# A CIN kernel on one Trainium2 core: the last stretch of matmuls put in another order, with other PSUM banks for two quadrant products

## The chip, the cores and the metric

The kernel runs on one core of a Trainium2 chip. The time is the device time of one execution in microseconds (us), and the median of several runs is compared. Beside these times there is one execution recorded by the profiler. Its engines are called PE (matrix multiplication; PEld are its weight loads), DVE (vector), ACT (scalar), POOL and SP (whose queue issues most of the loads).

## What is computed

The reference is a compressed interaction network over 1024 samples with 64 fields of 16 numbers each:

```python
x0 = h = x                                   # (1024, 64, 16)
for i in range(3):
    z = einsum('bfe,bge->bfge', x0, h)       # all products of two fields
    y = einsum('oc,bce->boe', W[i], z.reshape(B, -1, e)) + b[i]
    x_i, h = (y[:, :64], y[:, 64:]) if i != 2 else (y, y)
    xs.append(x_i)
return sum(concatenate(xs, 1), axis=2) @ fc_w.T + fc_b     # (1024, 1)
```

Everything is fp32. After the sum over the 16 numbers only one value for each sample is left, so the kernel folds the weights of the last layers with fc_w before the main loop. What remains for each sample and number e: h, the 64 upper outputs of layer 1, a sum over the products of fields x_f x_g with weights from W0; q, 64 sums over the same products with weights made from W1, W2 and fc_w; and smaller terms in x. The result is a sum over h times q and over the terms in x.

## The kernel before, in words

**Tiling.** The samples form 32 chunks of 32, so a chunk is 512 columns (32 samples by 16 numbers)[...]. The products of fields of a chunk are made as four blocks `z`, each 128 rows by 4 tiles by 512 columns (`product`, L237, and `w_product`, L631). A product multiplies `xa`, the chunk with shifted rows, by one quarter `xb` of another arrangement of it; for most products ACT first copies `xb` to a PSUM bank of the tag "y" (`second`, L551), of which there are two. PE multiplies 16 tiles of z by `w_all`, whose columns 0 to 63 give h and 64 to 127 give q. A matmul thus fills 64 output rows: half 0 is rows 0 to 63 of a bank, half 1 is rows 64 to 127. Two matmuls of different halves can run at a time. All main matmuls go through `mm`, L524, so the profile shows them at L525, told apart by their output's name.

**Stages.** Chunks 2, 3, 0 and 1 are the head, in which weights are still being made. Chunks 0, 1, 4 and 5 are finished plainly. Of chunks 2 and 3 only h is made there and kept in `hb`; their q is made at the end. Chunks 6 to 31 go as 13 pairs (`NPAIR`), numbered 3 to 15, in a scheme with seven half products instead of eight (Winograd's form of Strassen's): sums of blocks (T2, T3, B21, B22, X; on DVE and POOL) are multiplied by sums of weights (`ws`) into the banks alpha, delta (tag "acc", four banks) and beta (tag "set", two). Each pair is a window of 31 slots; a slot is a pair of 512-column matmuls.

**The last pair's leftovers.** A pair's window leaves over: one matmul into beta (`first_fill`, L715), eight of `late_run` and one with `vb` into alpha (L721), and four of `p4_run` into delta (L712, `LATE`). These run in the next pair's window. The last pair, number 15, has no next one, so they run in the stretch that the change touches, together with q of chunks 2 and 3. There, two of the eight late matmuls go to the free half of alpha's bank (`gamma`, L610) and are added later (`end_gamma`, L939).

**Quadrants.** For each chunk four smaller terms are taken by 64 by 64 matmuls, which use a quarter of the array each: `h_extra` (L564) and `v0x` (L571). For a pair this is `squares` (L725), at slot 30.2 of its window; for chunks 2 and 3 it is `end_squares` (L923). They read `e`, a chunk and its square (`square`, L179, on ACT).

**The end.** `end_q` (L912) multiplies the products of chunks 2 and 3 by the q weights into two banks: the first 384 columns (`ends[0]`, 24 samples) and, after them, the last 128 (`ends[1]`). Chunk 3 goes to half 0, chunk 2 to half 1. `end_extra` adds a term. DVE then finishes pair 15 (`end_pair`, L745: `w_hb`, `w_qa`, `w_ha`, twice `w_uu`, `x_v0x`, `sums`), adds up (`add_parts`, L947), and multiplies h by q of chunks 2 and 3 (`end_uu`, L933). PE sums over partitions with matmuls into `po` (`pools`, L953), placed in the middle of the 128-column matmuls; ACT and SP store the results. The last 8 samples of chunk 3 and of chunk 2 come last (L997 on).

**What sets the order.** The main part isn't written in order. `at(when, fn, ...)` (L515) puts a call into a list with a due time in slots, the list is sorted by it, and the calls then emit their instructions (L993). `zipped` (L518) gives two columns of jobs a slot for each row, the second column half a slot later. Each engine runs its own instructions in the order of emission; waits between engines, and for banks to become free, are put in by the framework. So the due times set an order, not times. In the end, `t` is the slot at which window 15 ends.

Of the kernel before, what the change touches and what calls it, by code (L numbers as in the profile page):

```python
# [37 lines left out]
F32 = mybir.dt.float32  # L38
# [8 lines left out]
N = CB * E  # L47
# [5 lines left out]
NT = NI * NJ  # L53
# [10 lines left out]
NPAIR = NCH // 2 - 3  # L64
GROUPS = [(j, i) for j in range(2) for i in range(NI)]
LATE = 4


@with_exitstack
def cin_kernel(ctx, tc, xra, xrb, wh, w0r, w1h, w2t, wx1, wx0, vec, out):  # L70
# [5 lines left out]
    ps = ctx.enter_context(tc.tile_pool(name="ps", bufs=2, space=bass.MemoryType.PSUM))  # L76
# [3 lines left out]
    def const_tile(name, shape):  # L80
        return const.tile(shape, F32, tag=name, name=name)
# [149 lines left out]
    hb = const_tile("hb", [128, NF // 2, N])  # L231
# [136 lines left out]
    for h in range(2):  # L368
        at = slice(32 * h, 32 * h + 32)
# [145 lines left out]
    def at(when, fn, *args, **flags):  # L515
        ops.append((when, len(ops), fn, args, flags))
# [7 lines left out]
    def mm(out, w, rhs, start=False, stop=False):  # L524
        nc.tensor.matmul(out, w, rhs, start=start, stop=stop, skip_group_check=True)  # L525
# [30 lines left out]
    def plain_product(when, c, j):  # L556
        at(when - 2.6, second, c, j)
        at(when, product, c, j, uses=NI)

    def q_extra(c, w, out=None):  # L560
        out = accs[c][halves[1 - c % 2]] if out is None else out[halves[c % 2]]
        mm(out, w, es[c])

    def h_extra(c, out=None, start=False):  # L564
        out = accs[c] if out is None else out
        mm(out[halves[c % 2]], w0ds[halves[1]], es[c][halves[1]], start=start)

    def new_y(k, tag):
        ys[k] = ps.tile([128, N], F32, tag=tag, name=f"y_{k}", bufs=4 if tag == "acc" else 2)

    def v0x(c, tag):  # L571
        if c // 2 not in ys:
            new_y(c // 2, tag)
        mm(ys[c // 2][halves[c % 2]], v0[halves[0]], es[c][halves[0]], start=True, stop=True)
# [47 lines left out]
    def w_run(p, out, w, name, start=False, at_t=0, order=GROUPS):  # L622
        return [
            (w_job, p, out, w, j * NI + i + at_t, name, start and n == 0)
            for n, (j, i) in enumerate(order)
        ]
# [85 lines left out]
    def p4_run(p):  # L712
        return w_run(p, delta, wh_all, "T2", at_t=2 * NI)

    def first_fill(p):  # L715
        return [(lambda: q_extra(p["a"], va, p["beta"]),)] + p4_run(p)[-LATE : -LATE // 2]

    def second_fill(p):
        return p4_run(p)[-LATE // 2 :]

    def late_run(p, out=alpha, first=0, last=2 * NI):  # L721
        jobs = w_run(p, out, s4, "B22", out is gamma)[first:last]
        return jobs if last < 2 * NI else jobs + [(lambda: q_extra(p["b"], vb, p["alpha"]),)]
# [8 lines left out]
    def window(t, p, fill, late, pad=[], order=GROUPS[NI:] + GROUPS[:NI], quads=30.2):  # L732
# [4 lines left out]
            w_run(p, delta, s3, "T3", True) + late + w_run(p, beta, wq_all, "B21", True, 2 * NI)  # L737
            + pad + p4_run(p)[:-LATE],
        )
# [5 lines left out]
    def end_pair(t, p, whens):  # L745
        hb_, qa, uub, ha, uua, xv, add = whens
        at(t + hb_, w_hb, p)
        at(t + qa, w_qa, p)
        at(t + uub, w_uu, p, alpha, "A", snaps[2])
        at(t + ha, w_ha, p)  # L750
        at(t + uua, w_uu, p, delta, "O", snaps[0])
        at(t + xv, x_v0x, p["k"])
        at(t + add, sums, p["k"])
# [79 lines left out]
    for n in range(NPAIR):  # L833
# [6 lines left out]
        t = T0 + SPAN * n  # L840
# [12 lines left out]
        else:  # L853
            q = pairs[-2]
# [46 lines left out]

    t, q = T0 + SPAN * NPAIR, pairs[-1]
    first, cuts = slice(0, CUT), (slice(0, E * CUT), slice(E * CUT, N))
    ends = []

    def new_ends():
        for n, cols in enumerate(cuts):
# [13 lines left out]
        mm(ends[n][halves[1 - c % 2]], va, es[c][:, cuts[n]])  # L921

    def end_squares():  # L923
        hx = ps.tile([128, N], F32, tag="set", name="hx")
        for c in (2, 3):
            h_extra(c, hx, True)
            v0x(c, "set")
        h = hb[:, 1, :]
        nc.vector.tensor_tensor(h, hx, h, ALU.add)
        for n in range(2):  # L930
            nc.scalar.copy(snaps[3][halves[1 - n]], h[halves[n]])
# [28 lines left out]
    for n in (2, 3):  # L960
        at(t - 34 + 6 * (n - 2), load_xa, n)
        at(t - 33.5 + 6 * (n - 2), load_xb, n)
        at(t - 13 + n / 10, load_e, n)
        at(t, square, n)
    at(t - 12, load_xx, 1)
    for when, c, j in ((-21.4, 2, 0), (-18.6, 3, 0), (-15.8, 2, 1), (-12.2, 3, 1), (-6.1, 2, 2), (-2, 3, 2)):
        plain_product(t + when, c, j)
    for when, c in ((-5, 2), (0, 3)):
        at(t + when, product, c, NJ - 1, engine=nc.gpsimd, uses=NI)
    end_pair(t, q, (0.7, 4.5, 13.8, 13.3, 13.5, 9.5, 14.5))  # L970
    at(t + 10.5, end_gamma)
    at(t - 0.1, new_ends)
    zipped(
        t,
        first_fill(q)[:1] + late_run(q, gamma, 0, 2) + [(end_q, 3, m, 0) for m in range(6)]
        + p4_run(q)[-LATE:] + [(end_q, 3, m, 0) for m in range(6, NT)] + [(end_extra, 3, 0)],
        [(end_q, 2, m, 0) for m in range(3)] + late_run(q, first=2)
        + [(end_q, 2, m, 0) for m in range(3, NT)] + [(end_extra, 2, 0)],
    )
    at(t + 9.9, end_squares)  # L980
    at(t + 15, x_v0x, 1)
    at(t + 15.1, sums, 1, of=slice(1, 2))
    t += 25
    at(t - 8, add_parts)
    at(t - 0.2, end_uu, 0)
# [96 lines left out]
```

## Time and profile before

| What | us |
|---|---|
| median of 3 runs | 453.62 |
| lowest and highest run | 453.42, 455.04 |
| the profiled execution, its own time | 453.26 |
| its span in the trace | 451.4 |
| PE busy in the span | 446.7 (99%) |
| DVE, POOL, ACT busy | 392.8, 364.7, 116.6 |
| one 512-column matmul row on PE (alpha<-z,ws), mean | 0.592 |
| one weight load of 64 columns, mean | 0.137 |

The granted clock of TensorE was 1.0. In the timeline, a row gives its start in us from the beginning of the span, its duration, engine, line, operation, output and inputs with their shapes, how often it occurs in direct succession (x2), and in brackets how long its engine was idle before it and what ended that. The duration of a MATMUL row is modelled and includes its way through the array, so rows of one half overlap; the distance between starts is what a matmul costs. Each fp32 matmul of the program appears as two MATMUL rows.

### The profile page before, as it was taken

What the parts mean: (1) busy time and instruction counts of PE and PEld (TensorE: products, weight loads), DVE (VectorE), ACT (ScalarE), POOL (GpSimd) and SP (SyncE); (2) the same over time, 40 slices, a digit from 0 to 9 for tenths busy, and PEclk for the clock granted to TensorE, in tenths of its full rate; (3) what the DMA queues carried; (4) which work ended last, traced back from release to release, by engine and by line L of the source; (5) the groups of instructions that cost most, each with busy time, mean ns of one, the idle gap of its engine ahead of it and who ended that gap; (6) DMA issues with size and microseconds to landing.
All of it is one profiled execution on the core that took longest, in us unless ns stands there. A gap on an engine that the chain in (4) does not pass through costs nothing.

```text
span 451.4 us, 6068 instructions
## 1 busy us (share of the span) xinstructions
PE 446.7 (99%) x2302; PEld 162.4 (36%) x2302; DVE 392.8 (87%) x284; ACT 116.6 (26%) x215; POOL 364.7 (81%) x125
## 2 busy tenths in 40 slices
PE   8999999999999999999999999999999999999997
PEld 4565343333333333333333333333333333333345
DVE  4995599998999998999999898999989899997833
ACT  3162251332313114131311413131131213125011
POOL 5423688999997979799797979989797998979900
DMA  8996998397949296794939679493967849490500
GB/s 308 407 313 152 335 384 355 126 319 195 303 95 350 83 272 237 150 352 90 340 107 266 236 164 337 95 346 102 268 226 177 325 103 353 139 278 25 118 0 2
DMA packets 34484, 99.67 MB, mean 221 GB/s; under 512 B 6324, under 2 KB 6996, under 8 KB 27864
## 3 DMA queue, kind: packets, MB, share of 16 engines
q1 hardware_dynamic: 31800, 84.70, 52.1%
q0 software_dynamic: 1872, 13.63, 16.7%
q10 hardware_dynamic: 784, 0.95, 0.8%
q8 instruction: 18, 0.29, 0.3%
q14 instruction: 10, 0.08, 0.0%
HBM read 84.00 MB, written 1.64 MB: 190 GB/s over the span
## 4 chain that ended last, share of the span: by engine, by line
PE 84%; DVE 10%; issue 3%; DMA 1%; SPq 0%; ACT 0%; ACTq 0%
PE alpha L525 51%; PE delta L525 10%; PE acc L525 7%; PE acc L251 6%; DVE z L633 5%; PE q L525 3%; PE acc L269 3%; PE beta L525 3%; DMA z<-in_w0r 1%; DVE acc L293 1%; DVE uu L289 1%; DVE uu L681 1%; DVE delta L678 1%; DVE xp L639 1%; PE y L525 0%
## 5 line engine op out<-in xcount | busy, mean ns | idle before, releaser
L650 POOL TENSOR_TENSOR z<-z,z 128x2048 f32<-128x2048 f32 (+1 forms) x78 | 300.0, 3881 | 29.5 <-PE alpha L525 29.3
L633 DVE TENSOR_TENSOR z<-xa,xp 128x2048 f32<-128x2048 f32 x103 | 231.6, 2279 | 1.2
L525 PE MATMUL alpha<-z,ws 128*64 128x512 f32 x624 | 220.7, 592 | 0.0
L525 PEld LDWEIGHTS alpha<-z,ws 128*64 128x64 f32 x624 | 69.5, 137 | 120.5 <-issue 118.6
L525 PE MATMUL delta<-z,w_all 128*64 128x512 f32 x208 | 95.8, 593 | 0.0
L553 ACT COPY xp<-xb 128x512 f32<-128x512 f32 x88 | 51.5, 588 | 164.2 <-DVE z L633 141.6
L525 PE MATMUL alpha<-z,w_all 128*64 128x512 f32 x208 | 91.9, 595 | 0.8
L525 PE MATMUL delta<-z,ws 128*64 128x512 f32 x208 | 91.9, 595 | 0.0
L525 PE MATMUL beta<-z,w_all 128*64 128x512 f32 x208 | 91.6, 593 | 0.0
L241 DVE TENSOR_TENSOR z<-xa,xp 128x2048 f32<-128x2048 f32 (+2 forms) x23 | 45.1, 2003 | 6.2 <-ACT xp L553 5.4
L525 PEld LDWEIGHTS alpha<-z,w_all 128*64 128x64 f32 x208 | 27.6, 137 | 59.1 <-issue 48.5
L241 POOL TENSOR_TENSOR z<-xa,xb 128x2048 f32<-128x2048 f32 x6 | 27.6, 4669 | 19.9 <-DMA xb<-in_xrb 19.9
L525 PEld LDWEIGHTS delta<-z,w_all 128*64 128x64 f32 x208 | 28.2, 137 | 29.2 <-issue 28.3
L251 PE MATMUL acc<-z,w_all 128*64 128x256 f32 x256 | 28.9, 381 | 0.6 <-DVE z L241 0.4
L525 PE MATMUL acc<-z,w_all 128*64 128x512 f32 (+1 forms) x96 | 29.4, 594 | 0.0
L525 PEld LDWEIGHTS delta<-z,ws 128*64 128x64 f32 x208 | 27.6, 137 | 4.6 <-issue 4.3
L525 PEld LDWEIGHTS beta<-z,w_all 128*64 128x64 f32 x208 | 27.8, 137 | 0.0
L664 ACT ACTIVATE snap<-alpha,vs 64x512 f32<-64x512 f32 x13 | 8.9, 683 | 55.7 <-PE alpha L525 55.7
L251 PEld LDWEIGHTS acc<-z,w_all 128*64 128x64 f32 x256 | 18.1, 137 | 12.9 <-DVE z L241 2.0
L525 PE MATMUL q<-z,w_all 128*64 128x384 f32 (+1 forms) x128 | 20.0, 382 | 0.0
L681 DVE SCALAR_TENSOR_TENSOR uu<-alpha,snap 64x512 f32<-64x512 f32 x13 | 9.0, 689 | 12.6 <-PE alpha L525 12.6
L661 ACT COPY snap<-alpha 64x512 f32<-64x512 f32 x13 | 7.6, 581 | 47.8 <-PE delta L525 45.4
(117 smaller groups left out, 365.0 us busy)
## 6 DMA issues: line engine op xcount, KB each, us to landing
xa<-in_xra SPq DMA_DIRECT2D x32, 1024.0 KB, 9.1
xb<-in_xrb SPq DMA_DIRECT2D x128, 256.0 KB, 7.9
z<-z POOLq DMA_DIRECT2D x13, 1024.0 KB, 9.4
e<-in_xra SPq DMA_DIRECT2D x28, 128.0 KB, 7.6
xx<-in_xra SPq DMA_DIRECT2D x28, 128.0 KB, 6.9
z<-in_w2t SPq DMA_DIRECT2D x2, 1024.0 KB
z<-in_wx SPq DMA_DIRECT2D x2, 1024.0 KB, 8.5
z<-in_w1h SPq DMA_DIRECT2D x1, 1024.0 KB
```

Of the source, the lines that this page charges most:

```text
L241: engine.tensor_tensor(blocks[zs[c, j]][:, at, :], xas[c][:, at, :], xbs[c][j].unsqueeze(1).to_broadcast([128, last - first, N]), ALU.mult,)
L251: nc.tensor.matmul(accs[c][halves[n]], w_all[:, t, 0:64], blocks[zs[c, j]][:, i, n * H2 : (n + 1) * H2], start=(t == 0), stop=(j == last a ...
L269: nc.tensor.matmul(accs[c][halves[1 - c % 2]], w_all[:, t, 64:128], blocks[zs[c, j]][:, i, :], start=(t == 0), stop=False, skip_group_chec ...
L289: nc.vector.scalar_tensor_tensor(uu[:, to, :], ys[k], cx, xxs[k], ALU.add, ALU.mult)
L293: nc.vector.tensor_reduce(acc[rows, of, k, half], uu[rows, of if at is None else at, E * half.start : E * half.stop].rearrange("p k (b e) ...
L525: nc.tensor.matmul(out, w, rhs, start=start, stop=stop, skip_group_check=True)
L553: nc.scalar.copy(bank, xbs[c][j])
L633: engine.tensor_tensor(blocks[b], xas[c], xbs[c][j].unsqueeze(1).to_broadcast([128, NI, N]), ALU.mult)
L650: nc.gpsimd.tensor_tensor(*(blocks[b][:, first:last] for b in (o, x, y)), ALU.subtract if in1 == "T3" else ALU.add,)
L661: nc.scalar.copy(snaps[0][p["O"]], alpha(p))
L664: nc.scalar.activation(snaps[1][p["O"]], alpha(p), AF.Identity, bias=bh1[p["A"]])
L681: nc.vector.scalar_tensor_tensor(uu[p[out], 0], x(p), 1.0 / QS, factor[p[out]], ALU.mult, ALU.mult)
```

## The change

It gives the matmuls of the last stretch another order, in which the two halves always have matmuls of equal size side by side, and takes the quadrant matmuls of chunks 2 and 3 to the place directly behind those of pair 15. There are the same matmuls as before, of the same sizes. In detail:

- Column 0 of the stretch was: beta, two gamma, six `end_q` of chunk 3, four of `p4_run` (delta), ten `end_q`, the extra. Column 1 was: three `end_q` of chunk 2, six late ones and `vb` (alpha), thirteen `end_q`, the extra. Now both begin with seven `end_q` (`FIRST`); then come seven of 512 columns in each (beta, two gamma and four delta; six alpha and `vb`), then nine `end_q` and the extra in each.
- `end_squares` is split. The matmuls come before the stretch (due at t - 0.7) and write to banks of the tag "y" instead of "set". The addition of h and its copies (`end_h`) stay at t + 9.9.
- So that the y banks are free, the last product on DVE (chunk 3, block 2) is due at t - 4.2 instead of t - 2, which takes it ahead of the `sums` of pair 14; and `square` of chunks 2 and 3 is due at t - 6 instead of t.
- The due times of pair 15's last steps follow the new order.

```diff
+FIRST = 7
...
-    ends = []
+    ends, hxs = [], []
...
     def end_squares():
-        hx = ps.tile([128, N], F32, tag="set", name="hx")
+        hx = ps.tile([128, N], F32, tag="y", name="hx")
+        hxs.append(hx)
         for c in (2, 3):
             h_extra(c, hx, True)
-            v0x(c, "set")
-        h = hb[:, 1, :]
+            v0x(c, "y")
+
+    def end_h():
+        hx, h = hxs.pop(), hb[:, 1, :]
         nc.vector.tensor_tensor(h, hx, h, ALU.add)
         for n in range(2):
             nc.scalar.copy(snaps[3][halves[1 - n]], h[halves[n]])
...
-        at(t, square, n)
+        at(t - 6, square, n)
     at(t - 12, load_xx, 1)
-    for when, c, j in ((-21.4, 2, 0), (-18.6, 3, 0), (-15.8, 2, 1), (-12.2, 3, 1), (-6.1, 2, 2), (-2, 3, 2)):
+    for when, c, j in ((-21.4, 2, 0), (-18.6, 3, 0), (-15.8, 2, 1), (-12.2, 3, 1), (-6.1, 2, 2), (-4.2, 3, 2)):
         plain_product(t + when, c, j)
...
-    end_pair(t, q, (0.7, 4.5, 13.8, 13.3, 13.5, 9.5, 14.5))
-    at(t + 10.5, end_gamma)
+    end_pair(t, q, (0.7, FIRST + 1.3, 14.9, 14.5, 14.7, 9.5, 15.4))
+    at(t + 14.2, end_gamma)
     at(t - 0.1, new_ends)
     zipped(
         t,
-        first_fill(q)[:1] + late_run(q, gamma, 0, 2) + [(end_q, 3, m, 0) for m in range(6)]
-        + p4_run(q)[-LATE:] + [(end_q, 3, m, 0) for m in range(6, NT)] + [(end_extra, 3, 0)],
-        [(end_q, 2, m, 0) for m in range(3)] + late_run(q, first=2)
-        + [(end_q, 2, m, 0) for m in range(3, NT)] + [(end_extra, 2, 0)],
+        [(end_q, 3, m, 0) for m in range(FIRST)] + first_fill(q)[:1] + late_run(q, gamma, 0, 2)
+        + p4_run(q)[-LATE:] + [(end_q, 3, m, 0) for m in range(FIRST, NT)] + [(end_extra, 3, 0)],
+        [(end_q, 2, m, 0) for m in range(FIRST)] + late_run(q, first=2)
+        + [(end_q, 2, m, 0) for m in range(FIRST, NT)] + [(end_extra, 2, 0)],
     )
-    at(t + 9.9, end_squares)
-    at(t + 15, x_v0x, 1)
-    at(t + 15.1, sums, 1, of=slice(1, 2))
+    at(t - 0.7, end_squares)
+    at(t + 9.9, end_h)
+    at(t + 15.6, x_v0x, 1)
+    at(t + 15.7, sums, 1, of=slice(1, 2))
```

In the compiled order, PE's instructions up to and including pair 15's quadrants, and all of ACT's, POOL's and SP's, are as before; DVE has the one swap of the last product with the sums of pair 14.

## The prediction

> **What bounds the kernel now.** I read the page first (busy shares, then the chain that ended last), then the timeline of the last 36 us, TensorE and VectorE together, because the change touches nothing before the last pair's quadrant matmuls.
>
> ```profile
> span 451.4 us, 6068 instructions
> ...
> PE 446.7 (99%) x2302; PEld 162.4 (36%) x2302; DVE 392.8 (87%) x284; ACT 116.6 (26%) x215; POOL 364.7 (81%) x125
> ...
> PE 84%; DVE 10%; issue 3%; DMA 1%; SPq 0%; ACT 0%; ACTq 0%
> ```
>
> PE is never without work. But a busy PE can have half of its columns idle: every matmul here fills 64 of 128 output columns, and two run side by side, one for output rows 0 to 63 (half 0), one for 64 to 127 (half 1). So the busy share cannot show what this change is about; the starts of single passes can (an fp32 matmul appears as two MATMUL rows, here called passes). The chain of the end is PE on every step until the last reduction and its store. The timeline, up to 432 us:
>
> ```profile
> 418.90 2.28 DVE L241 TENSOR_TENSOR z<-xa,xp 128x2048 f32<-128x2048 f32 x1
> ...
> 421.10 1.21 DVE L293 TENSOR_REDUCE acc<-uu 128x64 f32<-128x1024 f32 x1
> ...
> 422.23 2.28 DVE L241 TENSOR_TENSOR z<-xa,xp 128x2048 f32<-128x2048 f32 x1
> ...
> 423.53 0.64 PE L525 MATMUL alpha<-e,vs 64*64 64x512 f32 x1
> ...
> 424.55 0.64 PE L525 MATMUL beta<-e,va 128*64 128x512 f32 x1
> 424.56 0.86 PE L525 MATMUL q<-z,w_all 128*64 128x384 f32 x2
> 424.64 0.76 DVE L671 SCALAR_TENSOR_TENSOR snap<-alpha,vs,snap 64x512 f32<-64x512 f32 x1
> ...
> 425.46 0.54 PE L525 MATMUL q<-z,w_all 128*64 128x384 f32 x1
> 425.46 0.64 PE L525 MATMUL alpha<-z,ws 128*64 128x512 f32 x1
> ...
> 431.52 0.59 PE L525 MATMUL delta<-z,w_all 128*64 128x512 f32 x1
> ```
>
> And from there to the end:
>
> ```profile
> 431.95 1.02 PE L525 MATMUL alpha<-e,vb 128*64 128x512 f32 x2
> 432.90 0.64 PE L525 MATMUL hx<-e,vs 64*64 64x512 f32 x1
> ...
> 433.92 0.64 PE L525 MATMUL delta<-z,w_all 128*64 128x512 f32 x1
> ...
> 436.09 0.58 ACT L941 COPY snap<-alpha 64x512 f32<-64x512 f32 x1
> ...
> 436.70 0.71 DVE L942 TENSOR_TENSOR alpha<-alpha,snap 64x512 f32<-64x512 f32 x1 [1.91 <-ACT snap L941]
> ...
> 442.24 0.71 DVE L950 TENSOR_TENSOR acc<-acc 128x32 f32<-128x32 f32 x2
> ...
> 443.32 0.49 PE L525 MATMUL q<-e,va 128*64 128x384 f32 x1
> 443.64 2.13 PE L525 MATMUL q<-z,w_all 128*64 128x128 f32 x32
> 445.70 0.41 PE L872 MATMUL po<-acc,ones 128*2 128x32 f32 x12
> ...
> 448.15 0.22 PE L872 MATMUL po<-acc,turned 128*2 128x32 f32 x2
> 449.37 0.24 SPq L1010 DMA_DIRECT2D out<-hb  x1
> ```
>
> Three losses stand there. From 431.95 both passes of vb run on half 1 while half 0 has nothing (its delta ended at 431.95): 0.86 us of half an array. At 425.46 a q pass of half 1 starts together with alpha on half 0, although its forerunner was done at 425.25: it is issued behind that alpha and waits 0.21. In the last stretch half 1's 384 columns end at 443.06 and half 0's at 443.64; the 0.58 between is not recovered, as the pooling matmuls at 445.70 wait for both. Besides, the quadrant matmuls of chunks 2 and 3 (64*64, rows hx) stand alone and pay their own change of shape: 432.90 to 433.92 is 1.02, where two passes of 0.43 would be 0.86.
>
> **The change on PE, step by step.** The matmuls, their sizes and their number stay; only order and banks change. Passes: 512 columns take 0.4295 (alpha or delta starts 426.79, 427.23, 427.66 and so on), 384 take 0.3225 (q starts 428.83 to 431.09, seven passes in 2.26), so time goes with columns.
>
> Before, from the end of the last pair's quadrants: 424.55 to 432.90, 8.35; quadrants of 2 and 3, 1.02; 433.92 to 443.64, 9.72. Sum 19.09.
>
> After: the quadrants follow in the same shape, two passes, 0.86. Seven pairs of 384 are 14 x 0.3225 = 4.52, and 0.05 for the first pass after a change of shape (424.55 to 425.03 is 0.48, not 0.43). Seven pairs of 512 (beta, two gamma, four delta against six alpha and vb): 14 x 0.4295 = 6.01. Ten pairs of 384 (nine end_q and the extra): 20 x 0.3225 = 6.45. Sum 17.89. The difference is **1.20 us**. The rest is unchanged in order: 17 matmuls of 128 columns, pooling, 17 more, last sums, 443.64 to 451.4. They start at about 442.44 and all that follows moves by 1.20.
>
> Two rules bear on this. The Trainium skill, "TensorE: Matmul & The Clock Gate", Part 3 under The mechanism, says that a weight load overlaps a running matmul only where the row groups differ. All these matmuls use all 128 rows, so by the rule halves that end together would show each load, 0.137 (its row): 34 passes of 384 make 4.7 us, and the change would lose 3.5. The trace speaks against it: alpha and delta of 512 columns run in step from 398.49 to 405.41 at 0.43 a pass, loads of 0.14 inside, and the time per pass is proportional to columns, with no room for a fixed load. I take the row. And "TensorEngine Tiling (Array Packing)", Key Properties, lets tiles run independently of each other. By that the 0.21 at 425.46 would not exist, unequal neighbours would cost only at the ends, and the gain would be 1.0; the row shows the wait, so 1.20.
>
> **What moves beside PE.** The compiled order of ACT, POOL and SP is the same in both kernels, with the same z buffers; so the earlier `square` and every load cost nothing. VectorE has one swap: product (3, 2) goes ahead of the sums of pair 14. It would run 421.10 to 423.38: its buffer was last read by a POOL combination that ended at 418.76, its copied factor was written by 416.87. The sums then end at 424.59, and w_hb behind them started at 424.64 on alpha's own quadrants: nothing late.
>
> The swap is needed because hx and y of chunks 2 and 3 now take the two "y" banks, which hold the factors of products (2, 2) and (3, 2). That is the one added wait: PE's second quadrants, and behind them all that is left of PE's queue, wait for 423.38 but are due only at 424.44, so 1.06 to spare and cost 0. Without the swap it would end at 424.51 and cost 0.1. The old wait (banks of beta and y of pair 15) goes.
>
> The first q matmuls need products that ended by 416.23 and banks last read by 418.20. Delta needs the DMA issued by POOL at 418.66, which lands some 9.4 later (page), 428.1; delta is now due at 432.55. POOL's last product ends at 428.65, first read at about 439.2.
>
> VectorE's tail is where the gain could be caught. The copy of gamma on ACT (436.09) leads a chain of seven steps to 442.95, which the pooling matmuls need. In the changed order its wait stands behind vb, which now ends at 424.55 + 0.86 + 4.57 + 6.01 = 435.99 instead of 432.81. Before, ACT was late for another reason: it stood behind the copies of hb, which waited for hx. That goes: w_qa waits for beta to about 430.85, three steps of 0.7 follow, ACT's copies are over by 434.4. So gamma's copy starts at about 436.1 in both cases, the chain ends near 443.0, and PE reaches the pooling at 442.44 + 2.06 = 444.50. Its cover shrinks from 2.75 to 1.5: cost 0, and one for one beyond 1.5. The multiplication of q_0 and its sum come behind, over at 444.2; needed at 446.9.
>
> **Sum.** The profiled execution: span 451.4, time 453.26, 1.86 around it. Span 450.2, time 452.06. The median of the runs shown is 453.62, 0.36 above that execution, so I predict **452.4**, 0.26% less. A measurement of this kernel tells about 0.5% (2.27 us) from no change; this is under it.
>
> **Rivals.**
> - *The tail takes over* (0.10). Gamma's copy waits longer than read, or the reads of alpha and delta in PSUM are slowed. For: the cover is nearly halved, and PE's queue is in order. Against: every duration of the chain is measured, none changes. Late by 2.7 it returns the whole gain: 453.6.
> - *The quadrants wait in front of everything* (0.07), ending slower. If product (3, 2) is held to the end of POOL's next instruction (419.27 + 4.69 = 423.96), it ends at 426.24 and PE stands from 424.44 to 426.3: 1.86 lost, 1.20 won, 0.66 slower: 454.3. It decides from an end at about 425.6 on. Against: the buffer is free by 418.76 in the trace.
> - *Loads no longer hidden* (0.04), as the first rule has it: 453.6 + 3.5 = 457.1. Half of that would still be slower.
> - *More than the sum* (0.05). The two changes of shape around the pooling matmuls (0.2 each in the trace) shrink as well, or the medians scatter (453.42 to 455.04 before): 451.3.
> - *Forecast* (0.74), 452.4, itself between 451.8 and 453.1 by the scatter of the runs.
>
> The range of 451.4 to 454.0 leaves out the loads, the far part of the wait and the deepest gains. Faster by over 0.5% needs below 451.35: 0.06. Slower needs above 455.89, loads exposed or a wait of some 3.5: 0.06. Between: 0.88.
>
> **What the profile after would show.** Four hx and y rows per pass at about 424.44 and 424.87, no second change of shape; q at 425.41 with equal starts on both halves, 0.32 apart; vb in step with delta, at about 435.1; the first 128-column row near 442.4 and po near 444.5; hb's idle time gone from VectorE. The prediction is wrong if a gap stands ahead of hx (release by DVE), if 384-column passes in step take over 0.33, or if the po rows start right after L950 ends.

## The result and the profile after

| | before | after |
|---|---|---|
| median of 22 runs each, us | 454.10 | 452.96 |
| lowest and highest | 453.04, 455.48 | 452.17, 454.77 |
| profiled execution, span | 451.4 | 451.3 |

The ratio of the times is 0.9978, with a 95% interval from 0.9968 to 0.9989: 1.0 us less, between 0.5 and 1.5. The prediction was 452.4 and a difference of 1.20.

The two profiled spans differ by only 0.1, and the first thing to settle is why. In the page of the changed kernel the share of PE in the chain that ended last is smaller, although the change adds nothing to the chain:

```profile
span 451.3 us, 6067 instructions
...
PE 445.4 (99%) x2302; PEld 163.8 (36%) x2302; DVE 392.8 (87%) x284; ACT 116.6 (26%) x215; POOL 364.6 (81%) x125
...
PE 72%; DVE 15%; DMA 5%; issue 4%; POOL 3%; ACT 0%; DVEq 0%; POOLq 0%
```

The chain now leads back over waits far ahead of the change. The list of PE's waits over the whole span has one for a product in the head, and one for POOL's accumulating transfer, some 118 us after the start:

```profile
PE acc L252 <- DVE z L242: 1.3, 1, 1.3
...
PE delta L526 <- DMA z<-z: 0.5, 1, 0.5
```

In the kernel before, the first of these waits is 0.4 and the second isn't there; the code is the same in both kernels. Pair 15's quadrants start at 424.62 instead of 423.53, 1.09 later, before anything on PE that the change touches. So spans don't measure the change; what does is the stretch behind, whose length, as the second profile of the kernel before will show, doesn't move with its start. From here on **the closing stretch** is the time from the first quadrant row of pair 15 (alpha<-e,vs) to the first row of po<-acc,turned. Before, the two rows stand at 423.53 and 448.15: 24.62. The timeline of the changed kernel (rows of weight loads are left out here and below), first up to the end of the 512-column matmuls:

```profile
422.19 2.28 DVE L242 TENSOR_TENSOR z<-xa,xp 128x2048 f32<-128x2048 f32 x1
...
424.38 1.21 DVE L294 TENSOR_REDUCE acc<-uu 128x64 f32<-128x1024 f32 x1
424.62 0.64 PE L526 MATMUL alpha<-e,vs 64*64 64x512 f32 x1
...
425.10 0.59 PE L526 MATMUL alpha<-e,vs 64*64 64x512 f32 x1
...
425.53 0.60 PE L526 MATMUL hx<-e,vs 64*64 64x512 f32 x2
425.54 0.59 PE L526 MATMUL y<-e,v 64*64 64x512 f32 x2
...
425.73 0.76 DVE L672 SCALAR_TENSOR_TENSOR snap<-alpha,vs,snap 64x512 f32<-64x512 f32 x1
...
426.50 4.74 PE L526 MATMUL q<-z,w_all 128*64 128x384 f32 x28
431.06 0.59 PE L526 MATMUL beta<-e,va 128*64 128x512 f32 x1
431.07 0.59 PE L526 MATMUL alpha<-z,ws 128*64 128x512 f32 x1
...
436.64 0.59 PE L526 MATMUL delta<-z,w_all 128*64 128x512 f32 x1
436.65 0.59 PE L526 MATMUL alpha<-e,vb 128*64 128x512 f32 x1
```

And to the end:

```profile
437.29 0.58 ACT L945 COPY snap<-alpha 64x512 f32<-64x512 f32 x1 [1.95 <-PE alpha L526]
437.90 0.71 DVE L946 TENSOR_TENSOR alpha<-alpha,snap 64x512 f32<-64x512 f32 x1 [3.84 <-ACT snap L945]
...
443.42 0.72 DVE L954 TENSOR_TENSOR acc<-acc 128x32 f32<-128x32 f32 x2
443.52 2.13 PE L526 MATMUL q<-z,w_all 128*64 128x128 f32 x34
...
445.58 0.41 PE L873 MATMUL po<-acc,ones 128*2 128x32 f32 x12
...
448.02 0.22 PE L873 MATMUL po<-acc,turned 128*2 128x32 f32 x2
```

The closing stretch is 448.02 - 424.62 = 23.40: **1.22 less** (1.21 with a further digit), where 1.20 was predicted. The rows look as foretold: hx 0.43 behind the last quadrant pass without a gap, beta and alpha 0.01 apart, vb beside delta instead of alone, 128 columns starting at once on both halves, pooling 1.44 after the chain of VectorE has ended at 444.14.

So the sum was right. The question left for the runs: is it the equal sizes that bring it, as the prediction's steps have it? **Theory A**: the two halves run independently of each other; time is lost only where both must meet (at quadrants, at the pooling) and have not the same work behind them, where a matmul waits for another engine and holds up what is behind it, and at a change of shape. **Theory B**, the prediction's: matmuls start in program order, so unequal neighbours also hold each other up. (Program order is the order of emission: a slot's matmul of half 0, then that of half 1.)

### The profile page after: what moved, and what is told of

Its sections match the earlier page's. It is cut to its first block, busy times and chain, and to the rows that moved or that the text cites. A ratio compares the mean times of both kernels' runs of the same rounds, so it can differ in the third digit from the quotient of the medians.

```text
span 451.3 us, 6067 instructions
## 1 busy us (share of the span) xinstructions
PE 445.4 (99%) x2302; PEld 163.8 (36%) x2302; DVE 392.8 (87%) x284; ACT 116.6 (26%) x215; POOL 364.6 (81%) x125
## 4 chain that ended last, share of the span: by engine, by line
PE 72%; DVE 15%; DMA 5%; issue 4%; POOL 3%; ACT 0%; DVEq 0%; POOLq 0%
PE alpha L526 46%; PE delta L526 8%; DVE z L634 8%; PE acc L252 6%; PE q L526 3%; PE acc L270 3%; DMA z<-z 3%; PE beta L526 2%; DMA z<-in_wx 2%; POOL z L537 2%; DVE acc L294 2%; DVE uu L290 1%; DVE xp L640 1%; POOL z L242 1%; DVE uu L682 1%
## 5 line engine op out<-in xcount | busy, mean ns | idle before, releaser
L294 DVE TENSOR_REDUCE acc<-uu 128x64 f32<-128x1024 f32 (+2 forms) x19 | 19.6, 1036 | 0.2
```

The costliest lines, as they stand in the source:

```text
L294: nc.vector.tensor_reduce(acc[rows, of, k, half], uu[rows, of if at is None else at, E * half.start : E * half.stop].rearrange("p k (b e) ...
```

## The experiments

In the expectations "stretch" ends at the first 128-column row with which both halves are at work (20.11 before, 18.90 after); "to the last matmul" counts to the last matmul row in front of the final reduction (L1010 in the changed kernel), 0.61 behind po<-acc,turned (24.01 after). The table has the closing stretch as defined above, in which one profile can be held against another to 0.02. Where no time is given below, there is a single execution, and only its stretch is used.

| kernel | rows | closing stretch | against after |
|---|---|---|---|
| before, second profile | 424.13, 448.74 | 24.61 | +1.21 |
| quadrants moved, old sizes | 423.85, 447.25 | 23.40 | 0.00 |
| equal sizes only | 423.85, 447.57 | 23.72 | +0.32 |
| opposite sizes | 424.05, 447.46 | 23.41 | +0.01 |
| before, gamma one place later | 423.73, 448.09 | 24.36 | +0.96 |
| product twice | 424.42, 449.19 | 24.77 | +1.37 |
| sums twice | 424.10, 447.51 | 23.41 | +0.01 |
| sums three times | 426.13, 450.64 | 24.51 | +1.11 |
| pooling in the even place | 424.02, 447.22 | 23.20 | -0.20 |
| sums before the product | 425.36, 448.93 | 23.57 | +0.17 |

### The kernel before, profiled again

> The kernel before, unchanged, profiled once more. The profile of the changed kernel has pair 15's quadrants 1.09 us later than that of before (424.62 against 423.53), from waits for transfers in the head and at 118 us, in code that is the same. If that is scatter between executions, this profile has its quadrants anywhere from 423 to 426, but the stretch 20.11 again to 0.05. If it belongs to the change: 423.5 again.

Quadrants at 424.13, closing stretch 24.61 against 24.62. Its list of waits has 1.6 for a product in the head and 0.4 for the transfer. Over all profiles the quadrants stand between 423.53 and 426.13, with no clear relation to the kernel. The two latest, 426.13 and 425.36, are the two profiles with a granted clock of 0.91 in the first 20 us; the other ten lie within 1.09, still nearly the size of the effect. The stretch repeats to 0.01.

### One part at a time

The changed kernel with the old order of sizes, the quadrants staying where the change puts them:

```diff
-        [(end_q, 3, m, 0) for m in range(FIRST)] + first_fill(q)[:1] + late_run(q, gamma, 0, 2)
-        + p4_run(q)[-LATE:] + [(end_q, 3, m, 0) for m in range(FIRST, NT)] + [(end_extra, 3, 0)],
-        [(end_q, 2, m, 0) for m in range(FIRST)] + late_run(q, first=2)
-        + [(end_q, 2, m, 0) for m in range(FIRST, NT)] + [(end_extra, 2, 0)],
+        first_fill(q)[:1] + late_run(q, gamma, 0, 2) + [(end_q, 3, m, 0) for m in range(6)]
+        + p4_run(q)[-LATE:] + [(end_q, 3, m, 0) for m in range(6, NT)] + [(end_extra, 3, 0)],
+        [(end_q, 2, m, 0) for m in range(3)] + late_run(q, first=2)
+        + [(end_q, 2, m, 0) for m in range(3, NT)] + [(end_extra, 2, 0)],
```

The due times of pair 15's last steps went back with it.

> The changed kernel with the old order of sizes: only the quadrants of chunks 2 and 3 stay moved (with the y banks and the earlier product). Measured by the stretch from the first quadrant row of pair 15 to the first 128-column row of q: 20.11 us in the kernel before, 18.90 in the changed one. Theory A (the halves run independently; what cost time was that the quadrants stood in the middle of the stretch, where the halves were 0.86 apart, and one wait of 0.21 of a gamma matmul for w_hb on VectorE): 18.9 to 19.0, and the time of the changed kernel, about 0.25% under before. Theory B (my prediction's reading: matmuls start in program order, so unequal neighbours make each other wait): 0.64 more, 19.5, so about half of the gain.

```profile
423.85 0.64 PE L526 MATMUL alpha<-e,vs 64*64 64x512 f32 x1
...
442.75 2.13 PE L526 MATMUL q<-z,w_all 128*64 128x128 f32 x34
...
447.25 0.22 PE L873 MATMUL po<-acc,turned 128*2 128x32 f32 x2
```

From 423.85 to the first 128-column row at 442.75 are 18.90, as in the changed kernel to 0.01. Time 452.64 against 453.91, ratio 0.9964 (0.9949 to 0.9980). **The equal sizes contribute nothing here**; B's 0.64 is not there. Its chain on VectorE ends at 441.37 with the pooling at 444.81, so this version has a cover of 3.4 where the changed kernel has 1.44.

The kernel before with only the order of sizes (the due times of the last steps as in the change; the quadrants in the middle, a slot later than before, in the set banks):

```diff
-    at(t + 9.9, end_squares)
+    at(t + 10.9, end_squares)
...
-        first_fill(q)[:1] + late_run(q, gamma, 0, 2) + [(end_q, 3, m, 0) for m in range(6)]
-        + p4_run(q)[-LATE:] + [(end_q, 3, m, 0) for m in range(6, NT)] + [(end_extra, 3, 0)],
+        [(end_q, 3, m, 0) for m in range(FIRST)] + first_fill(q)[:1] + late_run(q, gamma, 0, 2)
+        + p4_run(q)[-LATE:] + [(end_q, 3, m, 0) for m in range(FIRST, NT)] + [(end_extra, 3, 0)],
...
```

> The kernel before with only the new order of sizes: the quadrants of chunks 2 and 3 stay in the middle of the stretch (after its eleventh slot) and in the set banks, the product behind the sums. Both halves then arrive at the quadrants together. Theory A: only the second change of shape is left, 0.21 us (1.02 for the quadrants instead of 0.86, and 0.05 on the first pass behind them): stretch 19.1, about 1.0 us under before. Theory B gives the same 19.1. If the neighbourhood of the quadrants and not the order were what counts: 20.1, no gain.

```profile
423.85 0.64 PE L526 MATMUL alpha<-e,vs 64*64 64x512 f32 x1
...
432.97 0.64 PE L526 MATMUL hx<-e,vs 64*64 64x512 f32 x1
...
443.06 2.13 PE L526 MATMUL q<-z,w_all 128*64 128x128 f32 x34
...
447.57 0.22 PE L873 MATMUL po<-acc,turned 128*2 128x32 f32 x2
```

To the 128-column row 443.06 - 423.85 = 19.21, expected 19.1; time 453.14 against 453.91, ratio 0.9982 (0.9968 to 0.9996). It has 0.90 of the 1.22. The expectation forgot the 0.09 that stand between the last pass ahead of the second quadrants and their first row (before: 432.81 to 432.90): a second change of shape costs 0.16 + 0.05 + 0.09 = 0.30.

So each part alone brings most of the gain, and they don't add up, because both cure the same thing: quadrants standing where the halves are apart. One takes the quadrants away, the other brings the halves together there.

### Sizes as unequal as can be

```diff
-        [(end_q, 2, m, 0) for m in range(FIRST)] + late_run(q, first=2)
+        late_run(q, first=2) + [(end_q, 2, m, 0) for m in range(FIRST)]
```

(w_hb's due time was moved ahead of this, so that it still reads alpha before the late matmuls add to it.)

> The changed kernel with sizes as unequal as they can be: half 1 begins with its seven 512-column matmuls while half 0 has seven of 384, then the other way round, then ten of 384 in both. The sum of each half is unchanged. Theory A: stretch 18.9 as in the changed kernel. Theory B: the starts in program order cost 0.64 and the stretch is 19.5. If the queue looks ahead by less than two matmuls, more than that, up to 1.5 (seven pairs at the price of the longer one, twice): 20.4.

442.95 - 424.05 = 18.90: no cost at all. Time 452.92 against 453.91, ratio 0.9975 (0.9962 to 0.9988). The timeline of this kernel shows how. In its program order vb of half 1 stands ahead of beta of half 0, and a q matmul of half 1 ahead of half 0's next one (alpha, here gamma's part):

```profile
430.50 0.59 PE L526 MATMUL beta<-e,va 128*64 128x512 f32 x1
...
430.92 0.59 PE L526 MATMUL beta<-e,va 128*64 128x512 f32 x1
431.17 0.59 PE L526 MATMUL alpha<-e,vb 128*64 128x512 f32 x1
431.35 0.59 PE L526 MATMUL alpha<-z,ws 128*64 128x512 f32 x1
431.60 0.59 PE L526 MATMUL alpha<-e,vb 128*64 128x512 f32 x1
...
432.03 0.49 PE L526 MATMUL q<-z,w_all 128*64 128x384 f32 x1
```

Beta starts 0.67 before vb, its forerunner in the program; gamma's matmul at 431.35 starts 0.68 before the q matmul at 432.03 that it follows. So a half does not wait for the start of the other half's matmul just ahead of it in the program.

Here a half never has to pass more than one such matmul. The kernel before has a place where it would be two, and there the half did wait:

```profile
443.06 0.38 PE L525 MATMUL q<-z,w_all 128*64 128x128 f32 x2
443.32 0.49 PE L525 MATMUL q<-e,va 128*64 128x384 f32 x1
443.64 2.13 PE L525 MATMUL q<-z,w_all 128*64 128x128 f32 x32
```

Half 1 starts its first 128-column matmul at 443.06, ahead of half 0's. At 0.109 a pass its second could start at 443.28, ahead of half 0's first two, but no row of half 1 starts before 443.64, where half 0's first one starts too; no wait for another engine is recorded there. The two other profiles with this order have the same step (443.65 and 444.24; 443.00 and 443.58). It costs nothing, since half 0 is the later one at the pooling. So independence is shown for a lead of one matmul, not more; whether a longer lead can cost time was not tried.

### What the 0.21 at 425.46 was

```diff
-        first_fill(q)[:1] + late_run(q, gamma, 0, 2) + [(end_q, 3, m, 0) for m in range(6)]
+        first_fill(q)[:1] + [(end_q, 3, 0, 0)] + late_run(q, gamma, 0, 2) + [(end_q, 3, m, 0) for m in range(1, 6)]
```

> The kernel before with one q matmul of chunk 3 put between beta and the first gamma matmul, so that this gamma matmul comes 0.65 us later, when w_hb on VectorE (which it must wait for, as both use alpha's bank) has ended. Theory A (the 0.21 at the second q matmul of half 1 was this wait, in front of it in PE's queue): the gap goes and the part up to the quadrants of 2 and 3 is 8.14 instead of 8.35, the stretch 19.9. Theory B (the 0.21 is the price of a start in program order behind the 512-column neighbour): nothing or little of it goes, 20.1.

The timeline of this kernel at that place:

```profile
424.75 0.64 PE L525 MATMUL beta<-e,va 128*64 128x512 f32 x1
424.75 0.86 PE L525 MATMUL q<-z,w_all 128*64 128x384 f32 x2
424.84 0.76 DVE L671 SCALAR_TENSOR_TENSOR snap<-alpha,vs,snap 64x512 f32<-64x512 f32 x1
...
425.23 0.59 PE L525 MATMUL beta<-e,va 128*64 128x512 f32 x1
425.45 1.13 PE L525 MATMUL q<-z,w_all 128*64 128x384 f32 x5
```

The second q matmul of half 1 starts 0.70 after the first one (before: 425.46 - 424.56 = 0.90), at once when its half is free, although its forerunner in the program, the inserted matmul of half 0, can start only behind beta's second pass (425.23 + 0.43 = 425.66). Quadrants to quadrants is 9.11 (432.84 - 423.73; before 9.37), the closing stretch 24.36, 0.26 less: the 0.21, and 0.05 for the first pass after it. So waiting for a busy half holds nobody else up here. What did, in the kernel before, was the wait for w_hb, which ended at 424.64 + 0.76 = 425.40, in front of the gamma matmul: the q matmul of the other half was queued behind that waiting instruction. In the changed kernel gamma comes after seven q matmuls and waits for nothing.

### The added wait and its price

The last product on VectorE written twice:

```diff
+    def again():
+        nc.vector.tensor_tensor(
+            blocks[zs[3, 2]], xas[3], xbs[3][2].unsqueeze(1).to_broadcast([128, NI, N]), ALU.mult
+        )
+
+    at(t - 4.1, again)
```

> The changed kernel with the last product on VectorE written twice, so that the y bank of its factor comes free 2.28 us later (the release that the second quadrants of chunks 2 and 3 wait for, with 1.07 us to spare in the changed kernel). If that wait has the price of the second rival in my prediction, one for one beyond the spare time: a gap of about 1.2 us ahead of the y or hx rows, the stretch 18.90 + 1.21 = 20.1, that is the time of the kernel before. If PE has other work to go on with or the release comes otherwise: 18.9.

```profile
424.31 2.29 DVE L974 TENSOR_TENSOR z<-xa,xp 128x2048 f32<-128x2048 f32 x1
424.42 0.64 PE L526 MATMUL alpha<-e,vs 64*64 64x512 f32 x1
...
425.34 1.02 PE L526 MATMUL hx<-e,vs 64*64 64x512 f32 x2
426.51 1.21 DVE L294 TENSOR_REDUCE acc<-uu 128x64 f32<-128x1024 f32 x1
426.65 0.64 PE L526 MATMUL y<-e,v 64*64 64x512 f32 x1 [0.29 <-DVE z L974]
```

The first hx matmul runs, y waits until 0.05 after the product's end at 426.60, and all behind it waits too. By its distance from the first quadrant row in the changed kernel, y was due at 425.34. Cost 1.37: 1.26 from there to the product's end, the 0.05, and 0.05 more for the first pass after the standstill come to 1.36. This shows the second rival's mechanism and price to be real; in the changed kernel it has not come to pass, since the product ended at 424.47 and y was due at 425.54.

The swap of the sums undone (`(-2, 3, 2)` instead of `(-4.2, 3, 2)`):

> The changed kernel without its swap on VectorE: the sums of pair 14 stay ahead of the last product, which then ends 1.13 to 1.2 us later and frees the y bank of its factor about 0.1 us after the quadrants of chunk 3 want it. Expected cost 0.1 by the wait alone, up to 0.25 if, as with the product done twice, part of the quadrants run ahead and the rest pay a first pass of their own: 24.1 to 24.3 from pair 15's first quadrant row to the last matmul, against 24.01.

```profile
424.06 2.28 DVE L242 TENSOR_TENSOR z<-xa,xp 128x2048 f32<-128x2048 f32 x1
...
426.39 0.64 PE L526 MATMUL y<-e,v 64*64 64x512 f32 x1
```

The product ends at 424.06 + 2.28 = 426.34, and y starts at 426.39 where 426.28 was due. Cost 0.17. The swap is needed, and worth that much.

### The cover of VectorE's tail

```diff
     at(t + 14.2, end_gamma)
+    for n in range(1):
+        at(t + 15.45 + n / 100, sums, q["k"])
```

> The changed kernel with the sums of pair 15 on VectorE done twice, 1.22 us more in the chain that ends ahead of the pooling matmuls. In the changed kernel it ends at 444.14 and the pooling begins at 445.58, 1.44 to spare. If my reading of the cover is right: no cost, the distance from the first 128-column row to the pooling rows stays 2.06.

> The same with the sums done three times, 2.44 us more. If the cover is 1.44: the pooling rows wait 1.0 to 1.1, the distance from the first 128-column row to them is 3.1 instead of 2.06, and the end comes that much later. If the pooling does not wait for this chain: 2.06. The kernel before had 2.75 of cover and would hide all of it.

With one more reduction the closing stretch is 23.41: hidden. With two (`range(2)`) it is 24.51, 1.11 more, as expected: the chain on VectorE ends 2.50 later after the quadrants, 1.06 beyond the cover of 1.44. The place differs a little from the expectation: pooling starts at 447.67, 2.64 behind the 128-column row and not 3.1, because its first matmul needs only the first of the two additions; the others wait once more.

```profile
447.44 0.71 DVE L954 TENSOR_TENSOR acc<-acc 128x32 f32<-128x32 f32 x2
447.67 0.22 PE L873 MATMUL po<-acc,ones 128*2 128x32 f32 x2 [0.51 <-DVE acc L954]
...
448.20 0.40 PE L873 MATMUL po<-acc,ones 128*2 128x64 f32 x10 [0.31 <-DVE acc L954]
```

(The span of this run, 453.9, says nothing of the edit: its quadrants stand at 426.13.)

### A further step

If meeting points are what counts, one is left: the pooling comes after nine 128-column matmuls of half 0 and eight of half 1.

```diff
-    at(t + 8, pools)
+    at(t + 8.6, pools)
```

> The changed kernel with one due time moved: the pooling matmuls come after nine 128-column matmuls of each half, not after nine of half 0 and eight of half 1. In the profile of the changed kernel half 1 has nothing for one matmul (two passes of 0.109) ahead of the pooling, and half 0 has nothing for as long behind it, since the pooling takes the whole array and both halves must wait for it. If only the point where both halves must meet counts, as the runs so far say: 0.22 us shorter from pair 15's first quadrant row to the last matmul (24.01 to 23.79), and a time 0.05% under the changed kernel, too little for the timed rounds to tell, about 0.3% under before. If the idle half there is filled otherwise: 24.01.

```profile
442.92 2.13 PE L526 MATMUL q<-z,w_all 128*64 128x128 f32 x36
...
447.22 0.22 PE L873 MATMUL po<-acc,turned 128*2 128x32 f32 x2
```

The closing stretch is 23.20, 0.20 under the changed kernel and 1.42 under the kernel before. Time 452.35 against 453.78, ratio 0.9975 (0.9961 to 0.9989): better than before; that it is better than the changed kernel only the stretch shows.

## Why the prediction was right, and which of its steps was not

**The sum on PE** held: 1.20 foretold, 1.22 in the profile, 1.0 (0.5 to 1.5) in the runs. Its terms, from the runs:

| term | us | shown by |
|---|---|---|
| quadrants in the middle with the halves apart (in passes, half 1 and half 0: 7.95 and 7.31 of work ahead of them, 9.03 and 9.67 behind; longer halves 17.62, balanced 16.98) | 0.64 | either part alone removes it; gamma one place later against equal sizes only, 24.36 - 23.72 |
| wait of gamma for w_hb, with half 1 queued behind it | 0.26 | gamma one place later |
| second change of shape for the quadrants | 0.32 | equal sizes only, against after |

**The step about start order failed.** The prediction took the 0.21 at 425.46 as the price of being issued behind a longer neighbour, and weighed that row against the rule of the Trainium skill ("TensorEngine Tiling (Array Packing)", Key Properties) that tiles run independently. The trace agrees with the rule as far as the runs reach: with the sizes set against each other the stretch stays at 18.90; the row at 443.06 shows that it has a limit. The row at 425.46 was read rightly as far as "behind alpha", but not why alpha was late: it started with beta's end, 425.46, and also 0.06 after w_hb's end, 425.40, and the prediction did not ask which. The sum came out all the same, because it used the measured 8.35, in which the wait was contained, and because the changed order does away with that wait too, by moving gamma. For these 0.26 that was luck: the prediction had them go because of the equal sizes.

**What the title says and what brings the time are not the same.** In the list of losses the prediction had the 0.86 of vb alone and the 0.58 at the end. They are one loss (0.64 in the sum) seen at its two ends, and it hangs on the quadrants' place. Moving them would have done, and would have kept more cover in VectorE's tail.

**Weight loads stay hidden.** Halves in step take 0.3225 for 384 columns: the 28 rows from 426.50 to 431.06 are 14 passes a half, 4.56, the 0.05 of the first included. So the rule of the Trainium skill that the prediction set aside ("TensorE: Matmul & The Clock Gate", Part 3, The mechanism), by which loads overlap only across row groups, does not hold for two column halves here; the same section also has loads go ahead into a background weight buffer, which no run here can tell.

**Beside PE** each cost put at nothing was nothing. The product ended 1.07 before y wanted its bank (1.06 foretold), w_hb was not late, the chain on VectorE ended 1.44 before the pooling (1.5 foretold). Both covers were measured by using them up: beyond them the cost is the lateness and about 0.1 more. The first rival had priced a return of the whole gain at a lateness of 2.7; the run with 2.5 more lost 1.11 of it, in line with that.

**The median** came out 0.5 above the predicted time; the kernel before, in 22 runs, was also 0.5 above its first three. That the head scatters by as much is shown by the profiles; that it made this 0.5 is likely, not shown.

## What to carry to other kernels

As long as a column half passes no more than one matmul of the other that has not started yet, it runs by itself, and what ties the two in these runs is a meeting point: matmuls of another shape, or an instruction that waits for another engine. Add up each half's work between meeting points; the loss comes from the difference there, and it is cured by moving the meeting point as well as by evening out the work. Where a change is smaller than the scatter of the rest of the kernel, measure the stretch between two rows that it cannot shift, and when a row starts late, compare the ends of all that it could have waited for before naming one.

## What was not expected of the hardware

- Matmuls of the two halves start out of program order: beta 0.67 ahead of its forerunner vb in the kernel with opposite sizes, though all of them go through one queue. A lead of two was not given in the kernel before: half 1 stood from 443.28 to 443.64.
- An instruction that waits for another engine blocks both halves: 0.21 for the other half in the kernel before, and everything behind y in the kernel with the product done twice.
- Standing apart from what follows, four quadrant matmuls cost 0.32 more than directly behind others of their shape, about as much as three quarters of a 512-column pass.
- The head of the same code took up to 2.6 us more in one profiled execution than in another, where the granted clock was 0.91 in the first 20 us of the slower one; at a full clock the profiles differ by up to 1.09.
